# Moving side steps of a two-layer attention kernel: convolution steps, one routing pass and the first keys

## The chip, the cores and the metric

The kernel runs on one core of one Trainium2 chip. The metric is device time in microseconds (us), the median of several runs of the same program. Engines are called by the profile's names: PE is TensorE's matmul, PEld its weight load, DVE VectorE, ACT ScalarE, POOL GpSimd, SP the engine that issues most DMAs.

## What is computed

The input x is 4 images of 128 channels by 64 x 64 places, in float32. Two layers follow each other.

```
# layer 0: attention over the 4096 places of an image, projections are 1x1 convolutions
e1, e2 = prelu(w1 @ gn(x) + b1), prelu(w2 @ gn(x) + b2)      # 64 rows each
asm    = prelu(wa @ gn(x) + ba)                              # 128 rows
x = x + softmax(e1^T e2) applied to asm
# layer 1: attention over the 4096 tokens of an image, then a mixture of experts
t = tokens(x)
t = t + softmax((ln(t) Wq^T)(ln(t) Wk^T)^T / 128) (ln(t) Wv^T)
# each of 64 experts takes, per image, its 8 best tokens by a softmax over tokens
p = softmax(ln(t) gate^T + gate_b, over the tokens);  vals, idx = top8(p)
pooled = sum over the 8 of vals * ln(t)[idx]
out_e  = gelu(pooled W1_e) W2_e
t[idx] += vals * out_e
```

gn is a group norm over 32 groups of channels, ln a layer norm over the 128 channels of a token.

## The kernel before

**Stages.** The work is laid out as eight stages, one for each image b and layer l, written (b, l), in the order (0,0), (1,0), (0,1), (2,0), (1,1), (3,0), (2,1), (3,1), and the expert part after them. A stage is `attention(b, layer)` (L532). It goes over 8 blocks of 512 queries and, in a block, over 8 groups of 512 keys, so a stage has 64 groups. A group makes the scores of two pairs of key tiles (`ps`, L551), takes their exponentials on ScalarE (`pt`, L560), then makes the products of the group before with the values (`av`: L485 in layer 0, L513 in layer 1). The products of a group are thus one group behind its exponentials. In layer 0, VectorE adds the exponentials up (`sacc`, L572 and L575). In layer 1, `mix` (L499 to L501) forms sums and differences of the exponentials on VectorE, three operations for each pair of tiles, so that fewer products are needed; L513 reads these (`tt`).

**Side steps.** Everything else is written as Python generators, and `stage` (L1035) hands each group one step of several of them: `step_after` (a step of the finishing of an earlier block), `coming` (the load and projection of the next block's queries, from group 1 on), `beside` (the side work of the stage), `packing` (expert weights). Steps of one group are an ordered neighbourhood: `tc.no_sync_barrier()` closes each group, and the compiler's scheduler orders the instructions of each engine between two of them. When a generator is exhausted, a chain goes on to the next.

**Finishing a layer-1 block** (`finish_attn`, L624) takes eight steps, groups 0 to 7 of the next block: (0) copies of `av` from PSUM on ScalarE and sums on VectorE; (1) the projection `pv` on TensorE into two tiles of the `ms` pool (L672), then the reciprocal `top_inv` (L678) and the scaled addition to the residual (L680); (2) a transpose; (3) the norm of the tokens (`norm_tokens`, L337, which has an inverse square root with a power on GpSimd, L182, between VectorE's L181 and L183), their store and a transpose; (5) loads; (7) the gate's logits `pg` (L739) and their 8 best (L752). In group 3 the next block's queries are projected too (`pq`, L454).

**The `ms` pool** has two PSUM banks. It is used by `pv`, `pq`, `pg`, by the convolution's `pe` and `pa`, by the group norm's products and by the routing's `pool`.

**The convolution** (`conv`, L253) makes keys, values and e1 of an image in layer 0. After one opening step it has three steps for each of 8 blocks: `pe` (L273; bias on ScalarE at L275; PReLU on VectorE at L232 and L234, in place in the tile `ye`; two DMAs that lay the key half out over both halves of the partitions, L279; a DMA of the other half to DRAM, L285), `pa` (L292, L298, PReLU), and an empty one. Image 0's convolution runs ahead of stage (0,0); for its first block the queries are made at once, by two more DMAs (`spread_query`, L247, L251). Image 2's convolution is beside stage (0,1), after a group norm of eight steps; image 3's is beside stage (1,1).

**The routing** (`route`, L830) of an image runs beside a later stage, once its last block is finished (`done_after`, L1023, waits nine steps). Its steps: the places of the 8 best by index search (L781); the replacement of the 8 best by a very small number in a copy z (L797) and a gather of the rows by four DMAs from GpSimd (L790); exponentials of the logits M in two steps (L845), in place, so after the replacement has read M; their sum and the weighted sum of the gathered rows; an empty step; a product into `pool` and the exponentials of z (L858) with the subtractions of z from M on GpSimd (L859), in two steps. Image 2's routing is beside stage (3,1), where in the first block of 64 groups another generator has the turn, so the nine steps begin with group 8. After it comes `first_weights`, whose first step is a guard's reductions (`watch`, L1754 to L1758), then loads of expert weights.

Of the kernel before, what the change touches and what calls it, by code (L numbers as in the profile page):

```python
# [15 lines left out]
P = 128  # L16
# [6 lines left out]
SCORE_COLS = {0: (slice(0, P),), 1: (slice(0, P // 2), slice(P // 2, P))}  # L23
# [3 lines left out]
def tile_unshifted(  # L27
# [15 lines left out]
    nc = tc.nc  # L43
# [4 lines left out]
    CR = a["w12T"].shape[1] // 2  # L48
# [3 lines left out]
    SUB = BLK // P  # L52
    NP = NJ // 2
    NG = NP // 2
# [25 lines left out]
    def block_tile(tag, name, bufs=2):  # L80
        pool = pools[of_pool.get(tag, "blk")]
        return pool.tile([P, BLK], F32, tag=tag, name=name, bufs=bufs)
# [45 lines left out]
    a12 = const.tile([P, 1], F32, tag="a12", name="a12")  # L128
    for i, al in enumerate(("a1", "a2")):
        nc.scalar.dma_start(  # L130
            out=a12[i * CR : (i + 1) * CR, :], in_=a[al].partition_broadcast(CR)
# [10 lines left out]
    for h in range(2):  # L142
# [15 lines left out]
        out=last, in_=last, compare_op=ALU.is_ge, fill=0.0, base=1 - P, pattern=[[0, P]],  # L158
# [9 lines left out]
        out=avg_g3, in_=avg_g3, compare_op=ALU.is_ge, fill=0.0, base=0,  # L168
# [3 lines left out]
        out=avg_g3, in_=avg_g3, compare_op=ALU.is_ge, fill=0.0, base=GS - 1,  # L172
# [57 lines left out]
    def prelu(outs, y, t, alpha):  # L230

        nc.vector.tensor_scalar(t, y, 0.0, alpha, op0=ALU.min, op1=ALU.mult)  # L232
        for o, part in outs:
            nc.vector.scalar_tensor_tensor(  # L234
                o, in0=part(y), scalar=0.0, in1=part(t), op0=ALU.max, op1=ALU.add
            )
# [10 lines left out]
    def spread_query(b, n, src):  # L247

        queries[b, 0, n] = q = block_tile("q", f"e1_{b}_{n}")
        for h in range(2):  # L250
            nc.sync.dma_start(out=q[h * CR : (h + 1) * CR, :], in_=src)  # L251

    def conv(b, whole=None, cols=(slice(0, P),)):  # L253


        kA = seq.tile([P, NP, P], F32, tag="k", name=f"e2_{b}")
        vT = seq.tile([P, NJ, C], F32, tag="v", name=f"asm{b}")
        keys[b, 0], values[b, 0] = kA, vT

        def block(n):  # L260
            if whole is None:
                return load_block("xs", x_of(b, n), f"ck{b}_{n}", 4)
            return whole[:, bass.ts(n, BLK)]

        xb = block(0)
        coming = normed(b, xb, f"xk{b}_0")
        xb = block(1)
        yield
        for n in range(NB):
            xn = coming  # L270
            pe = ms_tile(f"pe{b}_{n}")
            for part in cols:
                nc.tensor.matmul(pe[part, :], lhsT=w12[:, part], rhs=xn, start=True, stop=True)  # L273
            y, t = block_tile("ye", f"ye{b}_{n}"), block_tile("te", f"te{b}_{n}")
            nc.scalar.activation(y, pe, AF.Identity, bias=b12)  # L275
            prelu([(y, lambda z: z)], y, t, a12)
            y4 = y[CR:, :].rearrange("c (p h t) -> c p h t", h=2, t=P)
            for h in range(2):
                nc.sync.dma_start(  # L279
                    out=kA[h * CR : (h + 1) * CR, bass.ts(n, SUB // 2), :], in_=y4[:, :, h, :]  # L280
                )
            if whole is not None and n == 0:
                spread_query(b, n, y[:CR, :])
            else:
                nc.sync.dma_start(out=e1[b][n], in_=y[:CR, :])  # L285
            if n + 1 < NB:
                coming = normed(b, xb, f"xk{b}_{n + 1}")
            yield
            pa = ms_tile(f"pa{b}_{n}")
            for s in range(SUB):  # L290
                for part in cols:
                    nc.tensor.matmul(  # L292
                        pa[part, bass.ts(s, P)], lhsT=xn[:, bass.ts(s, P)][:, part], rhs=wa,
                        start=True, stop=True,
                    )
            y2, t2 = block_tile("ye", f"ya{b}_{n}"), block_tile("te", f"ta{b}_{n}")
            y3 = y2.rearrange("p (s c) -> p s c", c=C)
            nc.vector.tensor_tensor(  # L298
                y3, pa.rearrange("p (s c) -> p s c", c=C),
                ba.unsqueeze(1).to_broadcast([P, SUB, C]), op=ALU.add,  # L300
            )
            prelu(
                [(vT[:, bass.ts(n, SUB), :], lambda z: z.rearrange("p (s c) -> p s c", c=C))],
                y2, t2, aa,
            )
            if n + 2 < NB:
                xb = block(n + 2)
            yield
            yield
# [517 lines left out]

    QUARTERS = [bass.ts(i, S // 4) for i in range(4)]

    def route(b):  # L830

        hs = half_of(b)
        m = M[b // 2][hs, :]
        tot = small_tile("r_tot", b, 4)
        top, neg, at = places(b)
        yield
        z = seq.tile([P, S], F32, tag="k", name=f"z{b}")[hs, :]
        replace(b, top, z)  # L840
        got = block_tile("c0", f"got{b}")
        gather(b, at, got)
        yield
        for i, part in enumerate(QUARTERS):
            nc.scalar.activation(  # L845
                m[:, part], m[:, part], AF.Exp, bias=neg[hs, :], accum_out=tot[hs, i : i + 1]
            )
            if i % 2 == 1:
                yield
        nc.vector.tensor_reduce(tot[hs, 0:1], tot[hs, :], axis=AX.X, op=ALU.add)  # L850
        wgt = weights_of(b, top, neg, tot)
        halves = block_tile("c1", f"halves{b}")[:, :C]
        weigh(got, wgt, halves)
        yield
        yield
        pool_halves(b, halves, pooled)
        for i, part in enumerate(QUARTERS):
            nc.scalar.activation(z[:, part], z[:, part], AF.Exp, bias=neg[hs, :])  # L858
            nc.gpsimd.tensor_sub(m[:, part], m[:, part], z[:, part])  # L859
            if i % 2 == 1:  # L860
                yield
        if b == 1:
            nc.sync.dma_start(out=first_pair, in_=M[0])
# [155 lines left out]
    def idle(k):  # L1019
        for _ in range(k):  # L1020
            yield

    def done_after(gen):  # L1023

        yield from idle(NG + 1)
        yield from gen

    def chain(*gens):
        for g in gens:
            yield from g  # L1030
# [1 line left out]
    def query(b, layer, n):  # L1032
        return conv_query(b, n) if layer == 0 else attn_query(b, n)

    def stage(b, layer, beside, then, ahead=None, pace=(6, 3), hook=None):  # L1035

        coming = iter(())
        for k in range(pace[0]):  # L1040
            next(ahead or iter(()), None)
        for n, g in attention(b, layer):
            step_after()
            if g == 1:
                coming = query(b, layer, n + 1) if n + 1 < NB else then and query(*then, 0)
                coming = coming or iter(())
            next(coming, None)
            if n == 0 and ahead:
                for _ in range(pace[1]):
                    next(ahead, None)  # L1050
            else:
                next(beside, None)
            next(packing, None)
            if hook:
                hook(n, g)
            tc.no_sync_barrier()
        run(coming)
        run(beside)
# [26 lines left out]
    def first_weights():  # L1085

        watch(0)
        w1b = block_tile("xq", "w1b", 4)[:E, :]
        nc.sync.dma_start(out=w1b, in_=a["weight1"][:, D1 - 1, :])
        yield from idle(2)  # L1090
        new_place(6, seq, "k")
        new_place(2, extra, "w")
        for g in (6, 2):
            for h in range(2):
                load(g, g, h)
        yield from idle(2)
        pw = ms_tile("pw")
        for c in range(NHC):
            nc.tensor.transpose(
                pw[:, bass.ts(c, E)], w1b.rearrange("e (p c) -> e c p", c=NHC)[:, c, :],  # L1100
                ident[:E, :E],
            )
        nc.scalar.copy(w1bT.rearrange("p c e -> p (c e)"), pw[:, : NHC * E])
        yield from idle(2)
        new_place(7, seq, "v")
        for h in range(2):
            load(7, 7, h)
        yield

    def last_weights(n, g):  # L1110
# [4 lines left out]
        if n == NB - 1:  # L1115
# [7 lines left out]
    stage(0, 0, chain(group_norm(1), conv(1), weights_qk()), (1, 0), ahead=first_conv, pace=(4, 3))  # L1123
    packing = pack_weights()
    stage(1, 0, chain(group_norm(2), attn_keys(0), mix_values(0)), (0, 1))
    stage(0, 1, chain(group_norm(3), conv(2, cols=SCORE_COLS[1])), (2, 0))
    stage(2, 0, chain(done_after(route(0)), attn_keys(1), mix_values(1)), (1, 1))
    stage(1, 1, conv(3, cols=SCORE_COLS[1]), (3, 0))
    stage(3, 0, chain(done_after(route(1)), attn_keys(2), mix_values(2)), (2, 1))
    stage(2, 1, attn_keys(3), (3, 1))  # L1130
    ends["prep"].close()
    extra = ctx.enter_context(tc.tile_pool(name="extra", bufs=1, reuse_waits="tile"))
    stage(3, 1, chain(done_after(route(2)), first_weights()), None,
          ahead=mix_values(3), pace=(2, 1), hook=last_weights)
    products()
    keep_busy(FILL[0], "busy_a")
# [683 lines left out]
```

## Time and profile before

| | |
|---|---|
| median of 3 runs | 3289.64 us (3289.32 to 3291.17) |
| the profiled execution | 3289.95 us |
| its span, first to last instruction | 3288.2 us |
| mean granted TensorE clock | 0.996 |
| PE busy | 3230.3 us, 98% |
| DVE busy | 2118.7 us, 64% |
| ACT busy | 1253.1 us, 38% |
| POOL busy | 423.7 us, 13% |
| `ps`, L551, layer 1 / layer 0 | 929.2 / 490.6 us |
| `av`, L485 (layer 0) | 922.7 us |

A line of a timeline reads: start in us from the span's start, duration in us, engine, source line, operation, output<-input with partitions x elements, and the number of instructions merged. In brackets stands how long the engine was idle before it, and what released it. A line of the list of waits reads: the waiting engine and its operation, the operation waited for, then the total in us, how many times, and the longest. A line of the windows reads: the stretch and its length, the busy time of PE, PEld, DVE, ACT and POOL with their instructions, then the granted clock as a share of full speed, the DMA engines' busy share and GB/s. The chain is the work that ended last, followed back from the last instruction.

### The profile page before, as it was taken

Reading aid. Unit: us, or ns where it says so; the run is one execution under the profiler, and the core shown is the slowest. Engines: PE = TensorE matmul, PEld = TensorE weight load, DVE = VectorE, ACT = ScalarE, POOL = GpSimd, SP = SyncE. Lnnn points to the kernel's source line nnn. Section 1 sums busy time; section 2 is a strip of 40 time slices with the busy share of each in tenths; the row PEclk is TensorE's granted clock in tenths of the full one; section 3 lists DMA queues with packets and bytes.
Section 4 is the critical chain, followed back from the end, with each engine's and each line's share of the span. In section 5 each row is a group of like instructions: output and inputs, shape, how many; then the busy total and the mean of one; then the engine's idle time right before and its main releaser. Section 6 shows DMA issues by size and latency. Waiting matters only on the chain.

```text
span 3288.2 us, 49636 instructions
## 1 busy us (share of the span) xinstructions
PE 3230.3 (98%) x19856; PEld 1610.3 (49%) x19856; DVE 2118.7 (64%) x4189; ACT 1253.1 (38%) x1436; POOL 423.7 (13%) x414
## 2 busy tenths in 40 slices
PE   7999999999999999999999999999999999999996
PEld 4444444444655554444555554444444454444453
DVE  6665567556675667755675657775676566676565
ACT  3334434433333344333333334433333333433332
POOL 0111112310000004141000002241100002010011
PEclk9999999999999999999999999999999999999998
DMA  3221244232323222311121111321131111131149
GB/s 88 52 54 27 58 112 122 74 82 77 94 71 87 55 55 52 67 37 36 39 46 30 37 29 39 87 68 26 40 80 30 30 37 23 26 114 30 27 186 392
DMA packets 364689, 223.32 MB, mean 68 GB/s; under 512 B 273568, under 2 KB 298656, under 8 KB 359072
## 3 DMA queue, kind: packets, MB, share of 16 engines
q1 hardware_dynamic: 358992, 208.54, 23.7%
q10 hardware_dynamic: 4944, 10.46, 0.8%
q8 instruction: 158, 2.59, 0.3%
q0 software_dynamic: 512, 1.05, 0.1%
q14 instruction: 83, 0.68, 0.1%
HBM read 159.75 MB, written 97.19 MB: 78 GB/s over the span
## 4 chain that ended last, share of the span: by engine, by line
PE 96%; DVE 2%; DMA 0%; issue 0%; POOL 0%; ACT 0%; DVEq 0%; SPq 0%; ACTq 0%; POOLq 0%
PE ps L551 40%; PE av L485 27%; PE av L513 23%; PE pe L273 1%; PE pa L292 1%; PE pq L454 1%; PE pv L672 1%; PE ph L1171 0%; PE pg L739 0%; PE po L1201 0%; PE px L1265 0%; PE pd L599 0%; PE pht L1181 0%; DVE tt L499 0%; DVE w L1272 0%
## 5 line engine op out<-in xcount | busy, mean ns | idle before, releaser
L560 ACT ACTIVATE pt<-ps 128x1024 f32<-128x1024 f32 x1024 | 1020.6, 1024 | 1515.2 <-PE ps L551 1446.2
L551 PE MATMUL ps<-q,t 128*64 128x512 f32 x4096 | 929.2, 593 | 0.0
L485 PE MATMUL av<-pt,asm 64*128 64x512 f32 x4096 | 922.7, 589 | 0.9 <-ACT sw L643 0.9
L575 DVE TENSOR_TENSOR sacc<-sacc,pt 128x1024 f32<-128x1024 f32 x448 | 584.9, 1305 | 288.4 <-ACT pt L560 262.6
L513 PE MATMUL av<-pt,tt 128*64 128x256 f32 x3072 | 637.9, 380 | 0.0
L485 PEld LDWEIGHTS av<-pt,asm 64*128 64x128 f32 x4096 | 397.1, 187 | 484.4 <-issue 468.4
L499 DVE TENSOR_TENSOR tt<-pt 128x512 f32<-128x512 f32 x512 | 355.5, 694 | 371.8 <-ACT pt L560 355.2
L551 PEld LDWEIGHTS ps<-q,t 128*64 128x64 f32 x4096 | 315.3, 137 | 469.8 <-issue 442.4
L513 PE MATMUL av<-tt,mixed 128*64 128x256 f32 x2048 | 526.9, 380 | 5.4 <-DVE tt L499 5.4
L551 PE MATMUL ps<-e,e 64*128 64x512 f32 x2048 | 490.6, 596 | 2.9 <-DMA e<-ye 2.1
L513 PEld LDWEIGHTS av<-pt,tt 128*64 128x64 f32 x3072 | 359.9, 137 | 261.8 <-issue 137.9
L551 PEld LDWEIGHTS ps<-e,e 64*128 64x128 f32 x2048 | 193.1, 187 | 230.7 <-issue 225.5
L513 PE MATMUL av<-tt,tt 128*64 128x256 f32 x1024 | 305.1, 380 | 0.0
L513 PE MATMUL av<-pt,mixed 128*64 128x256 f32 x1024 | 305.1, 380 | 0.0
L513 PEld LDWEIGHTS av<-tt,mixed 128*64 128x64 f32 x2048 | 281.0, 137 | 9.7 <-DVE tt L499 6.3
L182 POOL TENSOR_TENSOR l_y<-l_v,mhalf 128x4 f32<-128x4 f32 x64 | 64.8, 1012 | 1586.4 <-DVE l_v L181 1586.0
L501 DVE TENSOR_TENSOR tt<-pt 128x256 f32<-128x256 f32 x512 | 220.6, 431 | 16.4
L500 DVE TENSOR_TENSOR pt<-tt,pt 128x256 f32<-128x256 f32 x512 | 218.5, 427 | 16.2
L513 PEld LDWEIGHTS av<-pt,mixed 128*64 128x64 f32 x1024 | 140.5, 137 | 61.2 <-DVE pt L500 0.3
L513 PEld LDWEIGHTS av<-tt,tt 128*64 128x64 f32 x1024 | 140.4, 137 | 2.1 <-DVE tt L501 0.5
L594 POOL TENSOR_TENSOR all_sum<-all_sum,c 128x512 f32<-128x512 f32 x32 | 44.9, 1402 | 520.7 <-DVE c L593 520.7
L183 DVE TENSOR_TENSOR l_z<-l_y 128x4 f32<-128x4 f32 x64 | 11.7, 183 | 96.6 <-POOL l_y L182 96.6
(265 smaller groups left out, 1791.9 us busy)
## 6 DMA issues: line engine op xcount, KB each, us to landing
wp<-in_weight_dram SPq DMA_DIRECT2D x128, 256.0 KB
w<-wp SPq DMA_DIRECT2D x22, 1024.0 KB
xq<-in_x_dram SPq DMA_DIRECT2D x32, 256.0 KB
rb<-inv SPq DMA_DIRECT2D x32, 256.0 KB
xT<-xt SPq DMA_DIRECT2D x128, 64.0 KB
ak<-xT SPq DMA_DIRECT2D x32, 256.0 KB
t<-kt SPq DMA_DIRECT2D x128, 64.0 KB
t<-t SPq DMA_DIRECT2D x32, 256.0 KB
```

Of the source, the lines that this page charges most:

```text
L182: nc.gpsimd.tensor_tensor(y[:, :k], v[:, :k], mhalf[:, :k], op=ALU.pow)
L273: nc.tensor.matmul(pe[part, :], lhsT=w12[:, part], rhs=xn, start=True, stop=True)
L292: nc.tensor.matmul(pa[part, bass.ts(s, P)], lhsT=xn[:, bass.ts(s, P)][:, part], rhs=wa, start=True, stop=True,)
L485: nc.tensor.matmul(avs[b, 0, n][:, r, :], lhsT=values[b, 0][rows, j, :], rhs=pt[rows, h, :], start=(j == 0), stop=(j == NJ - 1),)
L499: nc.vector.tensor_sub(tt[:, 0:2, :], p4[:, :, 1, :], p4[:, 0, :, :])
L500: nc.vector.tensor_add(p4[:, 0, 1, :], tt[:, 1, :], p4[:, 0, 0, :])
L501: nc.vector.tensor_sub(tt[:, 2, :], p4[:, 1, 0, :], p4[:, 0, 1, :])
L513: nc.tensor.matmul(av[bass.ts(half, HC), bank, slot, :], lhsT=lhsT, rhs=rhs, start=first, stop=final, skip_group_check=True,)
L551: nc.tensor.matmul(ps[part, h, :], lhsT=key[:, part], rhs=q[rows, :], start=True, stop=True,)
L560: nc.scalar.activation(pt, ps, AF.Exp, scale=scale)
L575: nc.vector.tensor_add(sums[b, n], sums[b, n], pt)
L594: nc.gpsimd.tensor_add(all_sum, all_sum, c1)
```

## The change

It has three parts. First, `stage` gets a parameter `skip`: in groups with that number the side work `beside` is not stepped. Stages (0,1) and (1,1), which have convolutions beside them, get `skip=1`. Their side work takes seven groups of a block instead of eight. Second, `route` gets a parameter `gap`, the number of further empty steps between the index search and the replacement with its gather, and `done_after` one for further steps ahead. Image 2's routing gets a gap of two and one step more ahead: the index search moves by one group, everything from the replacement on, and `first_weights` behind it, by three. Third, in the first block of image 0's convolution the last PReLU operation is done in three parts, with queries written to the query tile's first half and the two key halves to their places; a ScalarE copy makes the query tile's second half. The two key DMAs and the two query DMAs of that block go. All other blocks have their code as before.

```diff
@@ conv
+            places = [kA[h * CR : (h + 1) * CR, bass.ts(n, SUB // 2), :] for h in range(2)]
+            def chunks(h):
+                return lambda z: z[CR:, :].rearrange("c (p h t) -> c p h t", h=2, t=P)[:, :, h, :]
+            if whole is not None and n == 0:
+                queries[b, 0, n] = q = block_tile("q", f"e1_{b}_{n}")
+                prelu(
+                    [(q[:CR, :], lambda z: z[:CR, :])]
+                    + [(places[h], chunks(h)) for h in range(2)],
+                    y, t, a12,
+                )
+                nc.scalar.copy(q[CR:, :], q[:CR, :])
             else:
+                prelu([(y, lambda z: z)], y, t, a12)
+                for h in range(2):
+                    nc.sync.dma_start(out=places[h], in_=chunks(h)(y))
                 nc.sync.dma_start(out=e1[b][n], in_=y[:CR, :])
@@ route
-    def route(b):
+    def route(b, gap=0):
...
-        yield
+        yield from idle(1 + gap)
@@ done_after
-    def done_after(gen):
-        yield from idle(NG + 1)
+    def done_after(gen, more=0):
+        yield from idle(NG + 1 + more)
@@ stage
-            else:
+            elif g != skip:
                 next(beside, None)
@@ the stages
-    stage(0, 1, chain(group_norm(3), conv(2, cols=SCORE_COLS[1])), (2, 0))
+    stage(0, 1, chain(group_norm(3), conv(2, cols=SCORE_COLS[1])), (2, 0), skip=1)
-    stage(1, 1, conv(3, cols=SCORE_COLS[1]), (3, 0))
+    stage(1, 1, conv(3, cols=SCORE_COLS[1]), (3, 0), skip=1)
-    stage(3, 1, chain(done_after(route(2)), first_weights()), None,
+    stage(3, 1, chain(done_after(route(2, 2), 1), first_weights()), None,
           ahead=mix_values(3), pace=(2, 1), hook=last_weights)
```

More of the change, by code (lines that the diff above doesn't have):

```diff
@@ L275, in conv @@
             nc.scalar.activation(y, pe, AF.Identity, bias=b12)
[L276 to L280, printed above, removed]
-                )
-            if whole is not None and n == 0:
-                spread_query(b, n, y[:CR, :])
-            else:
+            places = [kA[h * CR : (h + 1) * CR, bass.ts(n, SUB // 2), :] for h in range(2)]
[7 more added lines that the diff above has]
+                    y, t, a12,
+                )
+                nc.scalar.copy(q[CR:, :], q[:CR, :])
+            else:
+                prelu([(y, lambda z: z)], y, t, a12)
+                for h in range(2):
+                    nc.sync.dma_start(out=places[h], in_=chunks(h)(y))
                 nc.sync.dma_start(out=e1[b][n], in_=y[:CR, :])
@@ L1033, in query, with stage @@
         return conv_query(b, n) if layer == 0 else attn_query(b, n)
-    def stage(b, layer, beside, then, ahead=None, pace=(6, 3), hook=None):
+    def stage(b, layer, beside, then, ahead=None, pace=(6, 3), hook=None,
+              skip=None):
         coming = iter(())
```

## The prediction

> **What bounds the kernel now.** I read the busy times and the chain first, then TensorE's list of waits over the whole span, then the timeline at each place that list led to.
>
> ```profile
> PE 3230.3 (98%) x19856; PEld 1610.3 (49%) x19856; DVE 2118.7 (64%) x4189; ACT 1253.1 (38%) x1436; POOL 423.7 (13%) x414
> PE 96%; DVE 2%; DMA 0%; issue 0%; POOL 0%; ACT 0%; DVEq 0%; SPq 0%; ACTq 0%; POOLq 0%
> ```
>
> TensorE is the bound: it is busy 98% of the 3288.2 us span, and 96% of the chain that ended last is its. The change removes no matmul, so it can only fill TensorE's 58 us of idle time and the slow clock after it. TensorE's list of waits (total, times, longest, us) has the part that the change can reach:
>
> ```profile
> PE av L513 <- DVE tt L499: 5.4, 2, 3.9
> PE pa L292 <- DVE top_inv L678: 4.7, 2, 2.4
> PE pe L273 <- DVE top_inv L678: 2.6, 1, 2.6
> ...
> PE ps L551 <- DMA e<-ye: 2.1, 1, 2.1
> PE ps L551 <- ACT ye L275: 0.8, 1, 0.8
> ```
>
> That is 15.6 us. The other waits lie ahead of the first key (10.9, 2.2), in the expert tail after 3190 us, or are under 1 us. Windows narrowed onto each put the L678 waits at 797, 918 and 1649 us, the L499 waits at 2865 and 2875, the last two at 20.8 and 27.5. The timeline shows the first:
>
> ```profile
> 795.82 1.05 PE L672 MATMUL pv<-wvd,u 128*64 128x129 f32 x16
> 799.50 1.30 PE L273 MATMUL pe<-xk,w 128*64 128x512 f32 x4 [2.63 <-DVE top_inv L678]
> 800.52 5.19 PE L551 MATMUL ps<-q,t 128*64 128x512 f32 x16
> ```
>
> The projection `pv` has taken both banks of the `ms` PSUM pool; the convolution's `pe`, a third in the same group, stands until VectorE has emptied one. VectorE reaches that (its L678 and L680 start at 798.21) only after six operations of the group's mixing. The next `ps` then takes 5.19 us instead of 3.60, and the windows there say why:
>
> ```profile
> 799.50:802.00 2.50, 2.50 (x8) 0.98 (x10) 0.82 (x3) 0.69 (x1) 0.00 (x0) 0.65 0.01 3
> 802.00:804.00 2.00, 2.00 (x8) 0.78 (x6) 1.36 (x3) 0.00 (x0) 0.00 (x0) 0.59 0.00 0
> ```
>
> The granted clock, third from the end, is 0.65 and 0.59. The stall near 2875 is VectorE's; its timeline there:
>
> ```profile
> 2870.81 0.17 DVE L181 TENSOR_SCALAR l_v<-l_mv 128x4 f32<-128x4 f32 x1
> 2875.77 0.16 DVE L183 TENSOR_TENSOR l_z<-l_y 128x4 f32<-128x4 f32 x1 [4.79 <-POOL l_y L182]
> ...
> 2878.35 0.65 DVE L499 TENSOR_TENSOR tt<-pt 128x512 f32<-128x512 f32 x1
> ```
>
> VectorE stands 4.79 us for a 1.05 us power on GpSimd, which sits behind the four gather DMAs of the routing (2869.87 to 2874.67). The mixing TensorE needs is queued behind that wait.
>
> **What the Trainium skill says.** "TensorE: Matmul & The Clock Gate", Part 1, has an idle TensorE fall to half clock, judged in free-running windows of about 3.4 us. The trace agrees: 2.63 and 3.92 us idle were followed by a low clock (0.65 and 0.59; 0.61 and 0.54), 2.34 and 2.36 us were not. The same page (Part 1, on queue depths) calls VectorE a strict FIFO, which is the 2875 case: exponentials lay ready from 2869.5 on. "SBUF — State Buffer", "Who interferes with whom", says that a VectorE operation with two SBUF inputs and a GpSimd operation that reads SBUF block each other for a whole instruction. It agrees: beside the routing's subtractions on GpSimd (L859, 2.45 to 2.58 us each), a 0.42 us mixing step at 2908.47 took 2.47 us. I use this for the cost of the routing's new place.
>
> **Part A, no convolution step in group 1.** Start to start of `ps`, an undisturbed layer-1 group takes 6.455 us (2847.10 minus 2840.65 is 6.45), `pv`, `pe` and `pa` 0.88 us each. At 789.36 two groups run to 809.41: 20.05 us against 6.455 + 0.88 + 0.88 and 6.455 + 0.88 (with the `pa` at 808.53), 15.55, so 4.5 lost (2.63 idle, the rest clock). At 911.02 one takes 10.77 against 8.21: 2.56. At 1641.59, 10.76: 2.55. Sum 9.6 us. Counting steps, both stages reach group 1 with a `pe` or `pa` exactly these three times; after the change never. What is late next? A convolution step in group 2 allocates a bank at the earliest 6.455 us later, near 803.3, where VectorE freed the first at 799.3: 4 us of cover. Before has `pe` in group 2 and `pa` in group 3 (steps 18 and 19 of stage (0,1)), beside `pq`, without a wait. The displaced steps bring their loads of x and stores of e1 on SP's queue up to five groups later (some 35 us); what they make is needed a stage later. The last `pa` of stage (0,1) is in group 36 of 64 instead of 31. Cost at nothing; without that cover, 2.55 a time. Gain 9.6; 8 to 9.6.
>
> **Part B, the routing of batch 2.** From 2854.44 to 2889.34 four groups take 34.90 us; the same groups one block on have (2971.99 to 2992.21, plus one of 6.455) 26.68. So 8.2 us hang here: 1.5 and 3.9 idle, some 0.9 of shorter waits, and clock. Index search (4.41 us) and replacement (4.40) move from groups 1 and 2 to 2 and 5. In group 2 VectorE is free about 3.3 us after the group's first `ps` (2975.3 against 2971.99); the search runs to +8.2, the norm of group 3 follows, and by the same durations group 3's mixing starts near +2 in group 4 and ends near +5, where TensorE needs its last part near +6.2. Tight, no stall. Replacement in group 5: group 6's matmuls need no norm; 4.40 + 3.1 of mixing is a little over one group, with no finishing step beside it. The gathers go with it, where GpSimd has no power to do. ScalarE's exponentials of M wait for the replacement and come after the exponentials of its group.
>
> Its tail moves too. The subtractions L859 now run in groups 7 and 0, where VectorE has idle of 2.6 to 3.1 us; three groups later they are in groups 2 and 3 of block 3, between mixing, `pv` evacuation and norm. Four times about 2.5 us (4.89 + 5.15 = 10.0) block VectorE. In block 4 the mixing of group 1 leads TensorE's need by about 5.3 us, later ones by about 6. The first pair eats that lead; walking on by hand, the second leaves mixing 1 us late and group 3's again 0.5. The bounds: 0 (the 1.5 us of the guard's reductions L1754 to L1758 move from group 1 of that block to group 4), and 10.0 − 5.3 = 4.7 plus 2 of clock, 6.7. I take 1.5, since in both pairs now one VectorE operation slips in between and no wait of TensorE follows. Net gain 6.7; 1.5 to 8.2.
>
> **Part C, first keys and queries.** Before: PReLU ends 19.03, two key DMAs and two query DMAs are issued from 19.05 to 21.72, `ps` starts at 22.95, TensorE idle 2.11. After: one 64x512 at 0.69 (nearest: L234 on 128x512), two of 64x256 at about 0.42 (nearest: L500), so keys at 19.9, and a ScalarE copy of 0.58 (nearest: L642) beside them. These 0.84 us of VectorE delay `ya` and so `pa` of block 1 (19.68 to 20.84) to 20.6 to 21.7. `ye` of block 1, which stood 5.78 us for the DMA to release its tile, comes 3 us earlier. The second group's keys still go by DMA: VectorE's eight steps up to that PReLU end near 23.5, plus the 2.25 us of now (25.99 to 28.24) 25.8; TensorE is through `pa` near 26.4. The second group's `ps` moves from 28.24 to about 26.4: 1.9 us. From there TensorE paces. Lower end 1.2 (only the first wait, `pa` ahead); upper 3.0 (idle 2.11 and 0.75 gone). No loss: the DMAs removed took longer than what replaces them.
>
> **Sum.** 9.6 + 6.7 + 1.9 = 18.2 us. The profiled execution took 3289.95 (span 3288.2 and 1.75 around it), 0.3 above the median of 3289.64; from the median, 3271.4.
>
> **The rivals.**
> 1. *GpSimd takes back what the routing gained*: near the 6.7 us bound. For it: the lock in the trace, and dense VectorE work in groups 2 and 3. Against: mixing is made a group ahead. Gain 9.6 + 1.9 + 1.5 = 13, time 3276.6.
> 2. *Slower, by the banks*: what waited in group 1 waits in group 2 or 3, where `pq` is a further user. Eleven `pe` or `pa` now fall there (five in stage (0,1), six in (1,1)); at 2.55 and, as in one of three now, 2 us of clock, some 3.2 each is 35 us: 3289.6 − 18.2 + 35 = 3306. It decides once six wait. Against: the 4 us of cover, and before's own steps in those groups.
> 3. *The spacing changes the order less than it says*: the compiler's scheduler orders within a group (the trace has the search of 2852.79 ahead of that group's mixing), and a search before mixing in group 2 still stalls there. Part B gives nothing and A loses one stall: 3289.6 − 7 − 1.9 = 3280.7.
> 4. *Nothing*: gains are met by new waits elsewhere, near 3288.
>
> **Chances.** Forecast (3268.5 to 3274) 0.60, rival 1 0.20, rival 3 0.09, rival 4 0.06, rival 2 0.05. The low end is all bounds at their best: 3289.6 − 9.6 − 8.2 − 3.0 = 3268.8, and 0.3 for the runs' spread below their median, so 3268.5; the high end reaches past rival 1 by its part C at 1.2 and part A at 8 (2.3 us less), so 3279. A measurement tells about 0.2% (6.6 us) from no change. Forecast, rivals 1 and 3 are faster by more: 0.89; same 0.06; slower 0.05.
>
> **What would show it.** Right: no wait of `pe` or `pa` for L678 (A); none of L513 for L499 near 2865 and 2875, L183's longest wait there back near 1.2 us (B); the first `ps` L551 near 21 us without a DMA wait (C). Wrong: `pe`, `pa` or `pq` waiting in groups 2 or 3; L513 waiting for L499 in block 3 of the last stage beside L859; a clock under 1 in either.

## The result, and the profile after

| | before | after |
|---|---|---|
| median | 3289.48 us (3288.63 to 3291.17, 4 runs) | 3269.18 us (3268.80 to 3270.16, 4 runs) |
| the profiled execution, and its span | 3289.95, 3288.2 us | 3268.95, 3267.2 us |
| mean granted clock | 0.996 | 0.997 |
| PE busy | 3230.3 us | 3227.5 us |

The kernel after is faster by 20.3 us: ratio 0.9939, with a 95% interval of 0.9927 to 0.9952. 18.2 us were forecast. (Lines after the edits have moved: `top_inv` is L687 now, mixing L508 to L510, `ps` L560, `av` of layer 1 L522, `pv` L681, the search L790, the replacement L806, the gather L799, the subtractions L868.)

First the busy times and the shares of the chain, after:

```profile
PE 3227.5 (99%) x19856; PEld 1544.2 (47%) x19856; DVE 2123.3 (65%) x4191; ACT 1255.6 (38%) x1437; POOL 425.4 (13%) x414
PE 97%; DVE 1%; DMA 1%; issue 0%; POOL 0%; ACT 0%; SPq 0%; ACTq 0%; DVEq 0%; POOLq 0%
```

TensorE's 19856 matmuls are the same ones, and it is still the bound. What shrank is the time in which it stands. Its list of waits over the whole span, after (total, times, longest):

```profile
PE gn_pm L214 <- DVE gn_mv L211: 10.6, 1, 10.6
PE pht L1192 <- DVE hp L1187: 2.4, 3, 0.8
...
PE pa L301 <- DVE ya L307: 0.5, 1, 0.5
...
PE ps L560 <- ACT ye L275: 0.5, 1, 0.5
```

The five lines that the prediction showed from this list are gone but for the last, which fell from 0.8 to 0.5. One line is new: at the start `pa` of the second block waits 0.5 us for VectorE, whose longer PReLU of the first block the prediction had named as what would delay it. What heads the list lies before the first key or in the expert tail, as it did.

**Where the first stall was**, TensorE's timeline and a window after:

```profile
793.41 1.05 PE L681 MATMUL pv<-wvd,u 128*64 128x129 f32 x16
794.29 3.60 PE L560 MATMUL ps<-q,t 128*64 128x512 f32 x16
...
800.74 3.60 PE L560 MATMUL ps<-q,t 128*64 128x512 f32 x16
```

```profile
802.00:804.00 2.00, 2.00 (x12) 0.72 (x10) 0.77 (x5) 1.02 (x1) 1.01 (x1) 1.00 0.70 230
```

No `pe` follows `pv` in its group; the next group's `ps` starts 6.45 us on; the clock (third from the end) is 1.00 where it was 0.59. `pe` now comes two groups later, at 808.06 behind `pq` (807.20), and waits for nothing.

**The routing**, VectorE and GpSimd after:

```profile
2854.07 1.01 POOL L182 TENSOR_TENSOR l_y<-l_v,mhalf 128x4 f32<-128x4 f32 x1 [56.81 <-DVE l_v L181]
2855.11 0.16 DVE L183 TENSOR_TENSOR l_z<-l_y 128x4 f32<-128x4 f32 x1 [1.12 <-POOL l_y L182]
```

The power L182 has GpSimd to itself and L183 waits 1.12 us for it, not 4.79. Search (4.41 us at 2845.78) and replacement (4.40 at 2863.44) take as long as before, but TensorE does not wait behind either.

**The start**, timeline after:

```profile
18.02 1.57 DVE L234 SCALAR_TENSOR_TENSOR e<-ye,te 64x512 f32<-64x512 f32 x3
...
21.46 1.99 PE L560 MATMUL ps<-e,e 64*128 64x512 f32 x8
...
25.85 2.09 PE L560 MATMUL ps<-e,e 64*128 64x512 f32 x7 [0.46 <-ACT ye L275]
```

Queries and both key halves are written by 19.6 (18.02 + 1.57), the copy on ScalarE runs beside them (18.74, 0.62 us), and the first `ps` waits for no DMA: it starts at 21.46, not 22.95.

**The gain place by place.** Both programs do the same work in nearly the same order, so the start of a marked matmul (`pd`, `pv`, `pq`, `pg`) before, minus its start in another kernel, is what that kernel has gained up to there. The marks below are at 86, 796, 1019, 2330, 2854 and 3186 us of the kernel before; the last is the last `pg`.

| kernel | start | 796 | after stage (0,1) | after (1,1) | ahead of the routing | last pg | profiled span | median of runs |
|---|---|---|---|---|---|---|---|---|
| after | 2.41 | 2.41 | 9.50 | 12.10 | 12.10 | 19.80 | 21.0 | 20.3 |

So stage (0,1) gave 7.09, stage (1,1) 2.60 (its marks just around the wait differ by 2.55), the routing 7.70 and the start 2.41, of which 0.31 is no gain of the change: the first `pe`, ahead of any edit, began at 14.67 instead of 14.98. The rest of the span's 21.0 us, 1.2, is in the expert tail behind the last `pg`, which took 100.8 us instead of 102.0. Over the kernels below that stretch takes 100.7 to 101.8 us, with nearly the same waits; no part of the change is seen in it.

### The profile page after: what moved, and what is told of

It reads as the page before. It is cut to its first block, busy times and chain, and to the rows that moved or that the text cites. A ratio compares the mean times of both kernels' runs of the same rounds, so it can differ in the third digit from the quotient of the medians.

```text
span 3267.2 us, 49620 instructions
## 1 busy us (share of the span) xinstructions
PE 3227.5 (99%) x19856; PEld 1544.2 (47%) x19856; DVE 2123.3 (65%) x4191; ACT 1255.6 (38%) x1437; POOL 425.4 (13%) x414
## 4 chain that ended last, share of the span: by engine, by line
PE 97%; DVE 1%; DMA 1%; issue 0%; POOL 0%; ACT 0%; SPq 0%; ACTq 0%; DVEq 0%; POOLq 0%
PE ps L560 41%; PE av L494 27%; PE av L522 24%; PE pe L273 1%; PE pq L463 1%; PE pv L681 1%; PE pa L301 1%; DMA tt<-x 1%; PE pg L748 0%; PE ph L1182 0%; PE pd L608 0%; PE po L1212 0%; PE pht L1192 0%; PE px L1276 0%; DMA first_x<-in_x_dram 0%
## 5 line engine op out<-in xcount | busy, mean ns | idle before, releaser
L560 PE MATMUL ps<-q,t 128*64 128x512 f32 x4096 | 924.8, 592 | 0.0
L522 PE MATMUL av<-pt,tt 128*64 128x256 f32 x3072 | 636.2, 379 | 0.0
L508 DVE TENSOR_TENSOR tt<-pt 128x512 f32<-128x512 f32 x512 | 354.2, 692 | 356.3 <-ACT pt L569 339.8
L522 PE MATMUL av<-tt,mixed 128*64 128x256 f32 x2048 | 525.6, 379 | 0.0
L560 PEld LDWEIGHTS ps<-q,t 128*64 128x64 f32 x4096 | 292.2, 137 | 489.2 <-issue 458.1
L522 PEld LDWEIGHTS av<-pt,tt 128*64 128x64 f32 x3072 | 353.9, 137 | 290.8 <-issue 143.4
L560 PE MATMUL ps<-e,e 64*128 64x512 f32 x2048 | 490.0, 596 | 0.5 <-ACT ye L275 0.5
L522 PE MATMUL av<-tt,tt 128*64 128x256 f32 x1024 | 304.7, 379 | 0.0
L522 PE MATMUL av<-pt,mixed 128*64 128x256 f32 x1024 | 304.6, 379 | 0.0
L560 PEld LDWEIGHTS ps<-e,e 64*128 64x128 f32 x2048 | 192.6, 187 | 228.1 <-issue 223.1
L522 PEld LDWEIGHTS av<-tt,mixed 128*64 128x64 f32 x2048 | 280.5, 137 | 2.7 <-DVE tt L508 0.2
L182 POOL TENSOR_TENSOR l_y<-l_v,mhalf 128x4 f32<-128x4 f32 x64 | 64.8, 1013 | 1612.6 <-DVE l_v L181 1612.3
L510 DVE TENSOR_TENSOR tt<-pt 128x256 f32<-128x256 f32 x512 | 220.4, 431 | 16.4
L522 PEld LDWEIGHTS av<-pt,mixed 128*64 128x64 f32 x1024 | 140.2, 137 | 72.9 <-DVE pt L509 0.3
L522 PEld LDWEIGHTS av<-tt,tt 128*64 128x64 f32 x1024 | 140.1, 137 | 1.5 <-DVE tt L510 0.3
L183 DVE TENSOR_TENSOR l_z<-l_y 128x4 f32<-128x4 f32 x64 | 13.9, 217 | 91.5 <-POOL l_y L182 91.5
```

Of the source, the lines that this page charges most:

```text
L182: nc.gpsimd.tensor_tensor(y[:, :k], v[:, :k], mhalf[:, :k], op=ALU.pow)
L508: nc.vector.tensor_sub(tt[:, 0:2, :], p4[:, :, 1, :], p4[:, 0, :, :])
L510: nc.vector.tensor_sub(tt[:, 2, :], p4[:, 1, 0, :], p4[:, 0, 1, :])
L522: nc.tensor.matmul(av[bass.ts(half, HC), bank, slot, :], lhsT=lhsT, rhs=rhs, start=first, stop=final, skip_group_check=True,)
L560: nc.tensor.matmul(ps[part, h, :], lhsT=key[:, part], rhs=q[rows, :], start=True, stop=True,)
```

## The experiments

The theory is the prediction's: three separate parts, each taking waits off TensorE. The rivals are that one part carries it or that the parts share gains; that a convolution step beside any projection would wait as well; that the gathers alone, not VectorE's long operations, made the routing's stall; and that GpSimd takes part of it back. The kernels of one group ran on one chip and share their runs of the kernel before.

### Each part alone

`a_only` keeps `skip=1` and undoes the rest, `b_only` keeps the routing's edit, `c_only` the first block's. The edits against the kernel after are two of these three each:

```diff
# undoing part A
-    stage(0, 1, chain(group_norm(3), conv(2, cols=SCORE_COLS[1])), (2, 0), skip=1)
-    stage(1, 1, conv(3, cols=SCORE_COLS[1]), (3, 0), skip=1)
+    stage(0, 1, chain(group_norm(3), conv(2, cols=SCORE_COLS[1])), (2, 0))
+    stage(1, 1, conv(3, cols=SCORE_COLS[1]), (3, 0))
# undoing part B
-    stage(3, 1, chain(done_after(route(2, 2), 1), first_weights()), None,
+    stage(3, 1, chain(done_after(route(2)), first_weights()), None,
# undoing part C
-            if whole is not None and n == 0:
+            if False:
...
-                nc.sync.dma_start(out=e1[b][n], in_=y[:CR, :])
+                if whole is not None and n == 0:
+                    spread_query(b, n, y[:CR, :])
+                else:
+                    nc.sync.dma_start(out=e1[b][n], in_=y[:CR, :])
```

> Part A alone (no convolution step in group 1; routing and first keys as before). Theory, three bank waits: 9.6 us less than before (4.5 + 2.55 + 2.55), no wait of pe or pa for the reciprocal of pv. Rival, that the parts hang together (the order that the scheduler writes after one moved step decides): not within 1 us of 9.6.

> Part B alone (routing of image 2 moved and spaced). Theory: 8.2 us hung on the routing and 0.5 come back as a short wait of the products for mixing in block 3 of the last stage, so 7.7 us less than before. Rival, the parts hang together: not within 1 us of 7.7.

> Part C alone (first keys and queries by engines). Theory: 2.1 us less than before, 2.4 if the start itself falls as in the run of the change; nothing else differs. Rival: as much as 3.3, since the tail of the profiled run of the change was 1.2 us shorter too and part C were its cause.

Before, beside them: 3289.43 us (3287.59 to 3291.62, 40 runs).

| kernel | median (range, runs) | ratio, 95% interval | gain by medians |
|---|---|---|---|
| a_only | 3280.21 (3279.05 to 3281.89, 8) | 0.9972, 0.9961 to 0.9982 | 9.2 |
| b_only | 3281.81 (3279.49 to 3283.84, 9) | 0.9976, 0.9966 to 0.9986 | 7.6 |
| c_only | 3286.88 (3284.85 to 3288.90, 13) | 0.9993, 0.9985 to 1.0002 | 2.55 |

| kernel | start | 796 | after stage (0,1) | after (1,1) | ahead of the routing | last pg |
|---|---|---|---|---|---|---|
| a_only | 0.10 | 0.10 | 7.19 | 9.80 | 9.80 | 9.84 |
| b_only | 0.03 | 0.03 | 1.72 | 1.70 | 1.70 | 9.40 |
| c_only | 1.90 | 1.90 | 3.59 | 3.56 | 3.56 | 2.23 |

The gains by medians add up to 19.4 us against 20.3 for all together, so the parts are separate. c_only's interval alone reaches past no change; the trace carries that verdict, not the time. By the marks, part A gives 9.70 (7.09 and 2.61), part B 7.70 exactly as in the whole, and part C 2.09: c_only's first `pe` began 0.19 us later than before's, and 1.90 + 0.19 is 2.09, as 2.41 − 0.31 is 2.10 in the whole change. The two kernels without part C set the margin of this: a_only gained 0.10 at the mark for a first `pe` 0.08 earlier, but b_only only 0.03 for one 0.31 earlier, so the 2.1 is known to about 0.3.

Two entries do not belong to the part that is named: b_only and c_only, which leave the first wait in place, gain 1.69 at it, and c_only loses 1.33 at the routing. The clock shows why. The first wait in c_only, and a window after it:

```profile
797.61 1.08 PE L273 MATMUL pe<-xk,w 128*64 128x512 f32 x4 [2.65 <-DVE top_inv L687]
798.49 3.63 PE L560 MATMUL ps<-q,t 128*64 128x512 f32 x16
```

```profile
799.00:802.00 3.00, 3.00 (x18) 1.21 (x16) 2.25 (x4) 1.44 (x2) 0.00 (x0) 1.00 0.00 0
```

The same in b_only:

```profile
799.49 1.08 PE L273 MATMUL pe<-xk,w 128*64 128x512 f32 x4 [2.65 <-DVE top_inv L690]
```

```profile
801.00:803.00 2.00, 2.00 (x12) 0.75 (x10) 1.64 (x3) 0.92 (x2) 0.00 (x0) 1.00 0.00 0
```

The wait is as long as before's, 2.65 us against 2.63, but no slow clock follows: `ps` takes 3.63 us in both, where before's took 5.19. At the routing's long wait, 3.92 us in both kernels, it is the other way round. Two windows of before, where that wait ended at 2879.05:

```profile
2881.00:2883.00 2.00, 2.00 (x16) 1.16 (x14) 1.95 (x4) 0.00 (x0) 0.00 (x0) 0.66 0.44 66
2883.00:2885.00 2.00, 2.00 (x13) 0.71 (x11) 1.81 (x8) 0.00 (x0) 0.00 (x0) 1.00 0.48 145
```

and two of c_only, where it ended at 2875.49:

```profile
2879.00:2881.00 2.00, 2.00 (x11) 1.12 (x9) 1.85 (x6) 0.00 (x0) 0.00 (x0) 0.50 0.25 50
2881.00:2883.00 2.00, 2.00 (x10) 0.56 (x8) 1.79 (x6) 0.00 (x0) 0.00 (x0) 0.88 0.74 262
```

Before's clock was full again 4 us after the end of the wait; c_only's was still 0.50 up to 5.5 us after it. So the same wait at the same place of the program can be followed by different clocks. What decides it is not shown. It is not the shift of the start, for b_only's first wait ended within 0.01 us of before's (799.49, 799.50). The Trainium skill ("TensorE: Matmul & The Clock Gate", Part 1) states free-running windows of about 3.4 us and a slow clock after at least one idle window. Windows that lie differently in each execution would fit what is seen here, but no run shows them, and before's slow clock came after 2.63 us of idle time, less than such a window. In these two profiles the three bank waits of part A therefore cost 9.6 − 1.7 = 7.9 us, of which 7.3 are idle, and in before's 9.6.

### A convolution step beside any projection?

`skip3` leaves out group 3 instead of group 1.

```diff
-    stage(0, 1, chain(group_norm(3), conv(2, cols=SCORE_COLS[1])), (2, 0), skip=1)
+    stage(0, 1, chain(group_norm(3), conv(2, cols=SCORE_COLS[1])), (2, 0), skip=3)
-    stage(1, 1, conv(3, cols=SCORE_COLS[1]), (3, 0), skip=1)
+    stage(1, 1, conv(3, cols=SCORE_COLS[1]), (3, 0), skip=3)
```

> The changed kernel, but the group left out in stages (0,1) and (1,1) is 3 instead of 1. By counting steps, four convolution matmul steps then fall in group 1 of a block whose predecessor is of layer 1 (the third pe and the last pa of stage (0,1), the third pa and the last pe of stage (1,1)). Theory, each such step waits for the banks: four waits of 2.3 to 2.7 us, 10.2 us slower than the change, 2 more for each wait that is followed by a low clock. Rival, that leaving out any one group in eight gives VectorE air and that is the gain: about the time of the change.

Median 3284.39 us (3279.93 to 3287.50, 21 runs), ratio 0.9986, 0.9980 to 0.9993: 15 us of the change's 20 are lost. The profiled execution was the fastest of these runs, 3279.93. Its list of waits:

```profile
PE pa L301 <- DVE top_inv L687: 4.8, 2, 2.4
PE pe L273 <- DVE top_inv L687: 4.7, 2, 2.6
```

Four waits, two in each stage, as counted (in stage (0,1) it is the fifth `pa` that waits, at 914.96, not the last, as the expectation has it). The marks are 4.21 after stage (0,1) where the change has 9.50, and the two stages together lose 10.3 (1.80 against 12.10 ahead of the routing): 9.5 are idle, and 0.8, some 0.2 a wait, are not in the list, as with before's second and third wait (2.56 and 2.55 lost, 2.34 and 2.36 idle). No slow clock followed in this execution. After each of the four waits the windows have 1.00, as this one after the first:

```profile
856.00:858.00 2.00, 2.00 (x12) 0.86 (x10) 1.80 (x3) 0.92 (x2) 0.00 (x0) 1.00 0.00 0
```

So it is group 1, with `pv` holding both banks, and not the spacing of steps as such. In the other runs up to 7.6 us more are lost. Four slow clocks of 1.7 to 1.9 us each would come to that; those runs left no trace that could show it, but the mean granted clock of each run goes with its time: five runs at 0.997 took 3281.5 us in the mean, eleven at 0.996 took 3284.9, and five at 0.995 took 3286.4.

### Which of the routing's moves counts

Three kernels order search, replacement and gather in other groups. Before: search 1, replacement and gather 2. After: search 2, both others 5. `replace_moved`: search 1, gather 2, replacement 5. `gather_moved`: search 1, replacement 2, gather 4. `gather_g3`: search 2, gather 3, replacement 5.

```diff
# gather_g3; replace_moved is the same with done_after(route(2, 3))
-        yield from idle(1 + gap)
+        yield
+        if gap:
+            got = block_tile("c0", f"got{b}")
+            gather(b, at, got)
+            yield from idle(gap)
...
-        got = block_tile("c0", f"got{b}")
-        gather(b, at, got)
+        if not gap:
+            got = block_tile("c0", f"got{b}")
+            gather(b, at, got)
# gather_moved, with done_after(route(2, 2))
-        yield from idle(1 + gap)
+        yield from idle(1)
...
         for i, part in enumerate(QUARTERS):
+            if gap and i == 2:
+                got = block_tile("c0", f"got{b}")
+                gather(b, at, got)
```

> The changed kernel with image 2's search back in group 1 and its gather in group 2, as before the change; only the replacement (and what must follow it) is in group 5. Theory 1, both stalls come of the replacement in group 2 (VectorE late by 4.4 us, and the gather's row copies and so the gathers held back behind it until they stand in front of the norm's power): no stall, the time of the change within 1 us. Theory 2, the gathers collide with the norm's power wherever they are issued in group 2: the 3.9 us wait and its slow clock stay, 5 us slower than the change.

> The changed kernel with image 2's search back in group 1 and its replacement in group 2, as before the change; only the gather moves, to group 4. Theory 1: the short wait for mixing near the replacement (1.5 us idle, 2.5 in all) stays and the long one goes, 2.5 us slower than the change. Theory 2 (gathers are the whole): the time of the change. Rival (the replacement delays ScalarE's exponentials, and that is the long wait): 8 us slower.

> The changed kernel, but image 2's gather is issued in group 3, the group of the norm, two groups ahead of the replacement. If gathers (about 5 us on GpSimd) stand ahead of the norm's power, VectorE waits for it and mixing comes late: with mixing about 2.5 us in hand at that place, 1 to 3 us slower than the change, and 2 more if the clock falls. If the rows are copied and gathered before the norm gets there: same time.

Before, beside them: 3288.44 us (3286.85 to 3291.43, 9 runs).

| kernel | median (range, runs) | ratio, 95% interval | routing's gain by the marks |
|---|---|---|---|
| replace_moved | 3270.69 (3270.30 to 3270.75, 5) | 0.9945, 0.9932 to 0.9959 | 18.60 − 11.75 = 6.85 |
| gather_moved | 3275.07 (3272.71 to 3279.42, 5) | 0.9961, 0.9948 to 0.9975 | 16.62 − 11.48 = 5.14 |
| gather_g3 | 3270.04 (3269.62 to 3270.14, 5) | 0.9943, 0.9930 to 0.9957 | 19.47 − 11.80 = 7.67 |

By the marks, theory 1 held for replace_moved (0.85 us less than the change's 7.70; by the medians it is 1.5 us slower) and for gather_moved (2.56 us less, 2.5 expected), and gather_g3 gained what the change gains.

In replace_moved the gathers (2851.22 to 2856.50) still stand ahead of the power (2856.53). VectorE there:

```profile
2857.61 0.16 DVE L183 TENSOR_TENSOR l_z<-l_y 128x4 f32<-128x4 f32 x1 [2.23 <-POOL l_y L182]
```

L183 waits 2.23 us, not 4.79: with no replacement between, the gathers were issued some 4 us before VectorE's L181 (2855.20) asked for the power. TensorE's list has one wait there, 0.3 us for mixing. In gather_moved the replacement keeps its place ahead of the mixing, and TensorE waits behind it:

```profile
2850.32 4.40 DVE L806 MATCH_REPLACE8 z<-r_top,M 64x4096 f32<-64x4096 f32 x1
...
2855.38 0.43 PE L522 MATMUL av<-tt,mixed 128*64 128x256 f32 x1 [1.50 <-DVE tt L508]
```

The 3.9 us wait is gone and the 1.5 us wait stays. (Its median is 2.4 us above its profiled execution, 3272.71, at the same mean clock; what the other runs lost is open.) So the long stall needed both: a replacement of 4.40 us that put the norm off, and gathers that by then were in GpSimd's queue ahead of the power. Either move alone ends it; only moving the replacement ends the 1.5 us wait too. Where the gather goes with the replacement parted from it hardly matters: in gather_g3 the power (2854.60) ran ahead of the gathers (from 2855.78), and the gain is the change's.

### The subtractions behind it

The change's routing still leaves something. At block 3 of the last stage, after:

```profile
2909.91 2.36 POOL L868 TENSOR_TENSOR M<-M,z 64x1024 f32<-64x1024 f32 x1
2909.96 2.33 DVE L183 TENSOR_TENSOR l_z<-l_y 128x4 f32<-128x4 f32 x1 [1.22 <-POOL l_y L182]
```

L183, 0.16 us elsewhere, takes 2.33 beside GpSimd's subtraction; the norm and the mixing behind it come late, three weight loads for L522 wait 0.23, 0.30 and 0.27 us for it, and the next group starts after 6.95 us instead of 6.45. `late_subs` puts the subtractions two groups later, `subs_far` five, into groups 7 and 0, where they were before the change; each has one of the two added lines.

```diff
         pool_halves(b, halves, pooled)
+        yield from idle(gap)            # late_subs
+        yield from idle(gap and 5)      # subs_far
         for i, part in enumerate(QUARTERS):
```

> The changed kernel with two more empty steps ahead of the exponentials of z, so that GpSimd's four subtractions of image 2 fall in groups 4 and 5 of block 3 instead of 2 and 3. Theory (the 0.5 us lost in block 3 is VectorE blocked beside the subtractions, in front of the norm): that wait goes, 0.5 us faster than the change. Rival (the 0.5 us belongs to the moved weight transposes): no difference.

> As the changed kernel, with five more empty steps ahead of the routing's exponentials of z and GpSimd's subtractions, and so ahead of the loads of expert weights behind them: the two pairs of subtractions fall in groups 7 and 0 of the block again, where they were before the change, while search, replacement and gather stay where the change has them. Theory (what the routing still costs is GpSimd's subtractions beside a dense VectorE; VectorE has room in groups 7 and 0): no wait of TensorE from L508 to L510 is left in the last stage, the routing gains 8.2 us over before instead of 7.7, median near 3268.7. Rival (the five groups' delay costs as much as it saves, by the guard's reductions or the weights behind): the routing gains 7.7 or less, median 3269.2 or above, and a wait shows after the subtractions.

late_subs: 3270.46 us (3269.78 to 3270.88, 5 runs), ratio 0.9945, 0.9931 to 0.9958; routing's gain 19.45 − 11.99 = 7.46, less than the change's 7.70. This expectation missed. VectorE's timeline there:

```profile
2915.42 2.49 DVE L509 TENSOR_TENSOR pt<-tt,pt 128x256 f32<-128x256 f32 x1
2917.95 2.47 DVE L510 TENSOR_TENSOR tt<-pt 128x256 f32<-128x256 f32 x1
2920.34 2.85 DVE L508 TENSOR_TENSOR tt<-pt 128x512 f32<-128x512 f32 x1
```

GpSimd ran all four in a row (10.17 us from 2912.46), and three mixing steps in a row took 2.47 to 2.85 us. TensorE waits 0.5 us for the third. The block moved; it did not go.

subs_far: 3269.05 us (3268.73 to 3269.66, 5 runs), ratio 0.9936, 0.9923 to 0.9950, beside a before of 3289.61 (3287.84 to 3292.13, 9 runs). No wait of TensorE is left between 2840 and 2995 us. The routing's gain is 19.88 − 11.25 = 8.63, 0.93 more than the change's and 0.4 more than expected. 0.50 of it is the group of 6.95 us. The other 0.43 is TensorE's own order, in one place of the change's trace:

```profile
2936.99 0.59 PE L748 MATMUL pg<-tg,gate 128*64 128x256 f32 x2
2937.20 0.59 PE L560 MATMUL ps<-q,t 128*64 128x512 f32 x1
2937.41 0.38 PE L748 MATMUL pg<-tg,gate 128*64 128x256 f32 x1
```

The four gate products lie among the last `av` and the first `ps`: from the first of them (2936.77) to the body of `ps` (2937.63) are 0.86 us. In subs_far's trace the four start together at 2937.11 and `ps` at 2937.54, 0.43 later. Before had such a place too, at 2902.25, where `pg` took 0.95 us up to the next product. Why the order differs was not tried. The median is only 0.13 us below the change's, within either kernel's range: a better order in the trace, but no time that tells. It is the fastest version by the medians here.

### Queries only

Of part C, `queries_only` keeps the queries in place and returns the first block's key halves to two DMAs.

```diff
                 prelu(
-                    [(q[:CR, :], lambda z: z[:CR, :])]
-                    + [(places[h], chunks(h)) for h in range(2)],
+                    [(y[CR:, :], lambda z: z[CR:, :]), (q[:CR, :], lambda z: z[:CR, :])],
                     y, t, a12,
                 )
+                for h in range(2):
+                    nc.sync.dma_start(out=places[h], in_=chunks(h)(y))
```

> As the changed kernel, but of the first convolution block only the queries are made in place; its two key halves go by DMA as before. Theory (the four DMAs came one behind the other, and the tile they read was held until the last had landed, so both halves of the edit count): two DMAs instead of four are left between PReLU and the first ps, which starts near 21.5 to 22 with a wait for a DMA in TensorE's list, against 22.95 before and 21.46 with the whole change; the tile ye is released about 2 us later than with the whole change, so the second block's keys and the second group's ps come later and the third group starts 1.0 to 1.5 us earlier than before instead of 2.4; median near 3270. Rival (the query DMAs alone were what the first ps waited for): the start is as with the whole change, third group 2.4 us earlier than before, median 3269.2.

3269.78 us (3269.59 to 3270.11, 5 runs), ratio 0.9938, 0.9925 to 0.9952. The start gains 1.77, or 1.59 with the first `pe`, 0.18 us earlier than before's, taken off: below the rival's 2.1, above my 1.0 to 1.5. Its timeline:

```profile
21.87 0.69 ACT L275 ACTIVATE ye<-pe,b 128x512 f32<-128x512 f32 x1 [1.66 <-DMA e<-ye]
...
26.48 2.10 PE L561 MATMUL ps<-e,e 64*128 64x512 f32 x7 [0.69 <-DMA e<-ye]
```

The first `ps` starts at 21.30, as early as with the whole change. So I was wrong on the first half: it was the two query DMAs, behind the key DMAs, that held it. The second half holds: the bias of the next block stands 1.66 us until the DMAs let go of `ye`, runs at 21.87, and the second group's `ps` waits 0.69 us. Queries in place give 1.6 of the 2.1 us, keys in place 0.5.

## Why the prediction was right, point by point

- **TensorE's idle time and the slow clock behind it are all that can be won**: right. The matmuls are the same, and the gain is 15.6 us of listed waits, less the 0.5 left, plus clock and small waits.
- **Part A, 9.6 us**: measured 9.69 in the change, 9.70 alone, so the counting of group lengths was exact for the profile it was made on; a_only's median gives 9.2. The prediction put 1.9 us of it down to the clock. What it did not say is that other executions need not lose these (b_only and c_only: 1.69 less); its low end of 8 is near the 7.9 that is left then. One step in group 1 was left out of its count, the first `pe` of stage (1,1) (1532.2 us), which stands behind a layer-0 block and does not wait. The displaced steps cost nothing, as said: `pe` behind `pq` at 808.06 has no wait. skip3 shows the price where cover is missing, 2.1 to 2.6 us each.
- **Part B, 8.2 us hang here, 1.5 come back, 6.7 net**: the mis-sized term. 7.70 were gained; the subtractions cost 0.50, not 1.5. The mechanism was the one named, and where: GpSimd's L868 against VectorE in block 3. The walk by hand put a block on mixing twice; in the run one pair lies on mixing that is made far enough ahead (2.47 us each near 2895 and no wait of TensorE), and of the second pair one subtraction lies on the norm. The 8.2 is borne out from the other side: with the subtractions away, subs_far gains 8.63, of which 0.43 is the gate products' order.
- **The walk through groups 2 to 5**: search and replacement bring no wait, as said. The scheduler put group 3's first mixing (from 2850.12, right behind the search) ahead of the norm, not after it, so there was more slack than in the walk.
- **Part C, 1.9 us**: 2.1. The first `ps` near 21 without a DMA wait: 21.46. `pa` of block 1 went from 19.68 to 20.37, near the 20.6 given, and the second `ps` from 28.24 to 25.85, 2.1 from the change and 0.3 from an earlier first `pe`. 26.4 was estimated.
- **The sum**: 9.6 + 6.7 + 1.9 = 18.2 stands against 9.7 + 7.7 + 2.1 = 19.5 by the parts and 20.3 by medians. The 1.0 us of part B is most of the first difference. The remaining 0.8 is not settled: it is less than the range of before's own runs (4.0 us over 40). All three terms were somewhat low and this went the same way, so the time lies only 0.7 us above the low end of the forecast, 3268.5.
- **The rivals**: GpSimd took back 0.5, not near 6.7. The banks made no new wait in groups 2 and 3; skip3 shows that rival's price was rightly set, but its place was wrong. The scheduler did not undo the spacing. The gains were not met by new waits, but for the 0.5 us of `pa` at the start.

## What to carry to other kernels

Here a third user of a two-bank PSUM pool cost its wait only in the group where the first two were filled; look for that group, and keep side work out of it alone, before spreading the work at large. When an engine stands behind another's queue, find both the thing that made it late and the thing that got in front: here moving either one ended the long stall, and moving the long operation ended the 1.5 us wait behind it too. What work on GpSimd costs VectorE depends on what VectorE has to do then: the same four subtractions cost TensorE nothing in groups with idle VectorE time and half a microsecond in dense ones.

## What the runs showed that I had not expected

- The same wait of 2.63 to 2.65 us was followed by a clock of 0.59 to 0.65 in one profile and of 1.00 in two others, a difference of 1.7 us. Kernels that keep such waits have wide ranges (before 4.0 us over 40 runs, b_only 4.35 over 9, c_only 4.05 over 13, skip3 7.6 over 21). Of those without them, a_only, which keeps the routing's waits, has 2.8 over 8, the change 1.4 over 4, and five others 0.45 to 1.1 over 5 each. gather_moved does not fit: its profile has none of these waits, only the one of 1.5 us, yet its five runs spread over 6.7 us, all at a mean clock of 0.997. Why is open.
- The small operation suffers as the large one does: VectorE's L183 on 128x4 elements took 2.33 us beside a subtraction of 2.36 us.
- In one place of two traces, four matmuls `pg` take 0.43 us up to the next `ps` where they stand together and 0.86 where they lie among others, so their order on TensorE has a price though none of them waits.
